# A four-layer graph network: VectorE's order in the last layers, the bias adds, and the exps of the last group of a chunk

## The chip, the core and the metric

The kernel runs on one core of one Trainium2 chip. The metric is the device time of one execution in microseconds (us); the profile is of one execution, taken by the hardware profiler. The engines are called PE (TensorE's matmuls) and PEld (its weight loads), DVE (VectorE), ACT (ScalarE), POOL (GpSimd) and SP (SyncE, which here only issues DMAs).

## The reference

A graph of 3327 nodes with 128 features, and a dense adjacency matrix `adj` (3327 x 3327). Four layers, each with a residual and a layer norm:

```python
# layer 0: attention, d = 128 features act as the batch, 8 heads inside, adj added to the scores twice
q = (x @ Wq.T).reshape(d, n, h); k = (x @ Wk.T).reshape(d, n, h); v = (x @ Wv.T).reshape(d, n, h)
a = softmax(einsum('dnh,dmh->dnm', q, k) * d ** -0.5 + adj + adj, axis=2)
x = layernorm(x + einsum('dnm,dmh->dnh', a, v).reshape(n, h * d) @ Wo.T)
# layer 1
dinv = sum(adj + I, axis=1) ** -0.5
x = layernorm(x + (dinv[:, None] * (adj + I) * dinv[None, :]) @ (x @ W1.T + b1))
# layer 2: rows of adj and of adj.T, each divided by its sum where that is positive
x = layernorm(x + norm(adj) @ x @ W_in + norm(adj.T) @ x @ W_out)
# layer 3
x = layernorm(x + x @ W_self.T + (adj @ x) @ W_neigh.T + b3)
```

## The kernel before, in words

**Attention** (0 to 9798 us of the profiled execution, after a set-up of some 320 us). The queries are cut into 7 chunks of 476 columns (`CW`), the keys into 4 key blocks of 7, 7, 6 and 6 tiles of 128 (`KBS`); one block of the program is one chunk with one key block, 28 in all. In each block a loop runs over the 128 features `d`, in groups of four (`GROUP`). A step of it makes the scores of one `d` in three sets of two or three key tiles: PE writes them to PSUM (`sc`, line 740), and `exponents` takes exp of them. ACT does most of it (line 745). Where `on_vector(b, d, si)` says so, the last tile of the set is left to DVE, which has no exp and does a chain of seven instructions instead (`vector_exp`, lines 630 to 647; the first, line 634, reads the scores from PSUM into `ey`). The table `SHARE` names the sets, by (3d + si) mod 36; 2072 of the 10752 sets have such a chain. `weigh` (line 780) multiplies the exps by the values; `flush` (line 794) adds the sums to `acc`. The orders of PE, ACT, POOL and DVE are written out in the source here (`tc.manual_schedule`): `take` decides, with costs and due times, which of DVE's pieces (first step of a chain, next step, flush, copy of queries) is traced next. In a chunk's first block DVE copies the queries of each group one group ahead (`copy_queries`, lines 538 to 540); for the first group this falls in the last group of the chunk before.

**The last layers** (9804 us to the end) work on 26 tiles `t` of 128 nodes.

- A first loop divides the attention's sums and projects them. `divide(t)` loads the tile `o` (SP), takes the reciprocal `rec` (DVE, line 1263) and multiplies it in (`on`, line 1265: POOL, DVE for t = 0). `stage0(t)` then has `heads_turned(t)` (8 transposes on PE, line 1273, copied by ACT), `outputs(t - 1)` (16 matmuls, line 1282; `h` on DVE, line 1285; the layer norm, with its last step on ACT), `turn(t - 3)` (a transpose, line 1214, copied by ACT) and `support(t - 4)` (the projection with `w1T`, line 1222, scaled by ACT into `y1`).
- Layer 1 gathers: for each `t` a tile `eT` of the transposed adjacency is loaded (1664 KB, five buffers) and 26 tokens' worth of matmuls, two each, accumulate in PSUM (line 1247). Between them, at fixed places, stand `turn(t - 1)` and `messages(t - 1)`, which need the norm of the tile before. Behind a gather come `z`, `h` and `norm` on DVE, then `add_columns(t)`: DVE sums the tile's columns (`part`, line 1229), from which layer 2's divisors are made.
- Layer 2 first multiplies by the adjacency itself (line 1353), then gathers again (10295 to 10478 us), with `back` and `last_inputs(t - 1)` between the matmuls; layer 3 gathers a third time and stores.

`project` adds the bias of layers 1 and 3 as a second matmul into the same PSUM bank: a row of ones against the bias row (line 1224; fp32 matmuls of this kind are issued as two instructions).

In the last layers `manual_schedule` names PE and SP: these two follow the source. The order of DVE, ACT and POOL is left to the framework's scheduler, so it can differ from the source's.

Of the kernel before, what the change touches and what calls it, by code (L numbers as in the profile page):

```python
# [10 lines left out]
F32 = mybir.dt.float32  # L11
# [3 lines left out]
ALU = mybir.AluOpType  # L15
# [4 lines left out]
P = 128  # L20
GROUP = 4
# [30 lines left out]
def kernel(ctx: ExitStack, tc: tile.TileContext, x, adj, wq, wk, wv, wo,  # L52
# [14 lines left out]
    nc = tc.nc  # L67
    N, D = x.shape
# [12 lines left out]
    KBS = [(0, 7), (7, 7), (14, 6), (20, 6)]  # L81
    assert KBS[-1][0] + KBS[-1][1] == T

    def tokens(t):
        return P - 1 if t == T - 1 else P

    def load_rows(eng, sb, dram, t):
        for a, n in spans(tokens(t)):
            eng.dma_start(out=sb[a:a + n, :], in_=dram[t * P + a:t * P + a + n, :])
# [5 lines left out]
    def flat_ap(dram, at, pattern):  # L95

        f = dram.rearrange("r c -> (r c)")
        if isinstance(at, int):
            base = f[at:at + 1]
        else:  # L100
            base = f[ds(at, 1)]
        return bass.AP(base.tensor, base.offset, pattern)

    const = ctx.enter_context(tc.tile_pool(name="const", bufs=1))
# [1 line left out]

    ident = const.tile([P, P], F32, name="ident")
    make_identity(nc, ident)
    ones_row = const.tile([1, P], F32, name="ones_row")
    nc.gpsimd.memset(ones_row, 1.0)  # L110
    eps = const.tile([P, 1], F32, name="eps")
    nc.gpsimd.memset(eps, EPS)

# [144 lines left out]
    with tc.tile_pool(name="pw", bufs=1) as pw, tc.tile_pool(name="pa", bufs=2) as pa, \  # L258
# [12 lines left out]
        for u in range(NU):  # L271
# [4 lines left out]
            for a, n in ([(0, P)] if full == P else [(0, 112), (112, full - 112)]):  # L276
                nc.sync.dma_start(out=xr[a:a + n, 0:R, :],
                                  in_=flat_ap(x, (base + R * a) * D, [[R * D, n], [1, R * D]]))
            if rest:
                nc.sync.dma_start(out=xr[full:full + 1, 0:rest, :],  # L280
                                  in_=flat_ap(x, (base + R * full) * D, [[D, 1], [1, rest * D]]))
            ps = pps.tile([P, 4, P], F32, tag="ps", bufs=3, name="xtr")
# [108 lines left out]
        d = 0  # L391
# [20 lines left out]
    def attention():  # L412
        with tc.tile_pool(name="ed", bufs=1) as ed, tc.tile_pool(name="kq", bufs=3) as kq, \
# [14 lines left out]
            blocks = [(min(c, N - CW), kb) for c in range(0, N, CW) for kb in range(len(KBS))]  # L428
# [3 lines left out]
            def load_edges(b, j):  # L432
# [15 lines left out]
            SHARE = {  # L448
                0: (8, 13, 20, 27, 32, 35),
                7: (5, 8, 12, 20, 23, 29, 32, 35),  # L450
                6: (4, 8, 13, 19, 25, 31, 35),
            }
# [25 lines left out]
            def kind(b):  # L478
                kb = blocks[b][1]
                return KBS[kb][1] if kb else 0  # L480

            def on_vector(b, d, si):
                return (3 * d + si) % 36 in SHARE[kind(b)]

            FIRST = {7: (4, 4, 5, 7, 7, 10, 10), 6: (4, 4, 7, 7, 10, 10)}

# [659 lines left out]
    act = ctx.enter_context(tc.tile_pool(name="act", bufs=1))  # L1146
    small = ctx.enter_context(tc.tile_pool(name="small", bufs=4))
    big = ctx.enter_context(tc.tile_pool(name="big", bufs=5))
    work = ctx.enter_context(tc.tile_pool(name="work", bufs=3))
    banks = ctx.enter_context(tc.tile_pool(name="banks", bufs=1, space=PSUM))  # L1150
    xs = [act.tile([P, T, D], F32, name=f"x{i}") for i in range(2)]
    y1 = act.tile([P, T, D], F32, name="y1")
# [3 lines left out]
    def bank(i):  # L1156
        return banks.tile([P, 512], F32, tag=f"bank{i}", name=f"bank{i}")

    w1T, w2, w3T, woT = (act.tile([P, w], F32, name=f"tw{i}") for i, w in enumerate((D, 2 * D, 2 * D, HD)))
# [1 line left out]
        nc.scalar.dma_start(out=sb, in_=dram)  # L1161
    nc.scalar.dma_start(out=w2[:, 0:D], in_=w2_in)
    nc.scalar.dma_start(out=w2[:, D:2 * D], in_=w2_out)
    b1_sb = act.tile([1, D], F32, name="b1_sb")
    nc.scalar.dma_start(out=b1_sb, in_=b1.unsqueeze(0))
    b3_sb = act.tile([1, D], F32, name="b3_sb")
    nc.scalar.dma_start(out=b3_sb, in_=b3.unsqueeze(0))


    for i in range(4):  # L1170
# [3 lines left out]
    dinv = act.tile([P, T], F32, name="dinv")  # L1174
# [33 lines left out]
    xTs = {}  # L1208
# [6 lines left out]
        xTs[t] = work.tile([P, P], F32, name="xT")  # L1215
        nc.scalar.copy(xTs[t][:, :n], ps[:, :n])

    def project(t, w, bias, b):

        n = tokens(t)  # L1220
        ps = bank(b)
        nc.tensor.matmul(ps[:n, 0:w.shape[-1]], lhsT=xTs[t][:, :n], rhs=w, start=True, stop=bias is None)  # L1222
        if bias is not None:
            nc.tensor.matmul(ps[:n, 0:D], lhsT=ones_row[:, :n], rhs=bias, start=False, stop=True)  # L1224
        return ps

    def add_columns(t):
# [39 lines left out]
    def heads_turned(t):  # L1267
        n = tokens(t)
        oTs[t] = work.tile([P, H, P], F32, name="oT")
        for c in range(0, H, 4):  # L1270
            ps = bank(c // 4).rearrange("p (c n) -> p c n", n=P)
            for i in range(4):
                nc.tensor.transpose(ps[:, i, :n], ons[t][:n, c + i, :], ident[:n, :n])  # L1273
            nc.scalar.copy(oTs[t][:, c:c + 4, :n], ps[:, :, :n])
# [12 lines left out]

    def support(t):
        n = tokens(t)
        ps = project(t, w1T, b1_sb, 5)  # L1290
        nc.scalar.mul(y1[:n, t, :], ps[:n, 0:D], dinv[:n, t:t + 1])

    def messages(t):
        n = tokens(t)
        ps = project(t, w2, None, 5)
        nc.scalar.copy(y2[:n, t, :], ps[:n, 0:2 * D])

    def last_inputs(t):
        n = tokens(t)
        ps = project(t, w3T, b3_sb, 5)  # L1300
        nc.vector.tensor_tensor(xs[1][:n, t, :], ps[:n, 0:D], xs[0][:n, t, :], ALU.add)
        nc.scalar.copy(y3[:n, t, :], ps[:n, D:2 * D])

    with tc.manual_schedule(engines={mybir.EngineType.PE, mybir.EngineType.SP}):
        def stage0(t):
            if t < T:
                heads_turned(t)
            if 1 <= t <= T:
                outputs(t - 1)
            if 3 <= t <= T + 2:  # L1310
                turn(xs[0], t - 3, 4)
            if 4 <= t <= T + 3:
                support(t - 4)

        for t in range(T):
            divide(t)
            stage0(t)


        def after(src, t, finish):  # L1320
            return [(12, lambda: turn(src, t, 4)), (19, lambda: finish(t))] if t >= 0 else []

        for t in range(T):
            n = tokens(t)
            ps = gather(t, y1, 0, 6 + t % 2,
                        after(xs[1], t - 1, messages) if t else
                        [(2 + 5 * k, lambda k=k: stage0(T + k)) for k in range(4)])
            z = work.tile([P, D], F32, name="z")
            nc.vector.tensor_tensor(z[:n, :], ps[:n, 0:D], y1[:n, t, :], ALU.add)
            h = work.tile([P, D], F32, name="h")  # L1330
            nc.vector.scalar_tensor_tensor(h[:n, :], z[:n, :], dinv[:n, t:t + 1], xs[0][:n, t, :],  # L1331
                                           ALU.mult, ALU.add)
            norm(n, h[:n, :], xs[1][:n, t, :])
            add_columns(t)
        inv_col = inverse_degree(colsum, "inv_col")


        backT = act.tile([P, NP], F32, name="backT")
        cols = [(c, min(512, N - c)) for c in range(0, N, 512)]
        order = [6, 0, 1, 2, 3, 4, 5]  # L1340
        acc = {}
        for t in range(T):
            n = tokens(t)
            a = big.tile([P, T * P], F32, tag="big", name="a2")
            load_rows(nc.sync, a[:, 0:N], adj, t)
            for i, (c, w) in enumerate(cols):
                if t == 0 and i == 3:
                    turn(xs[1], T - 1, 4)
                if t == 0 and i == 5:
                    messages(T - 1)  # L1350
                if t == 0:
                    acc[i] = bank(order[i])
                nc.tensor.matmul(acc[i][:, 0:w], lhsT=y2[:n, t, D:2 * D], rhs=a[:n, c:c + w],  # L1353
                                 start=(t == 0), stop=(t == T - 1))
        for i, (c, w) in enumerate(cols):
            copy(i, backT[:, c:c + w], acc[i][:, 0:w])


        for t in range(T):
            n = tokens(t)  # L1360
            zs = {}

            def back(t=t, n=n):
                pb = bank(t % 2)
                nc.tensor.transpose(pb[:n, 0:P], backT[:, t * P:t * P + n], ident)
                zs[t] = work.tile([P, D], F32, name="z")
                nc.vector.scalar_tensor_tensor(zs[t][:n, :], pb[:n, 0:D], inv_col[:n, t:t + 1], xs[1][:n, t, :],
                                               ALU.mult, ALU.add)

            ps = gather(t, y2, 0, 7 - t % 2, [(6, back)] + after(xs[0], t - 1, last_inputs))  # L1370
            h = work.tile([P, D], F32, name="h")
            nc.vector.scalar_tensor_tensor(h[:n, :], ps[:n, 0:D], inv_row[:n, t:t + 1], zs[t][:n, :],  # L1372
                                           ALU.mult, ALU.add)
            norm(n, h[:n, :], xs[0][:n, t, :])


        for t in range(T):
            n = tokens(t)
            ps = gather(t, y3, 0, 6 + t % 2, after(xs[0], T - 1, last_inputs) if t == 0 else ())
            h = work.tile([P, D], F32, name="h")  # L1380
            nc.vector.tensor_tensor(h[:n, :], ps[:n, 0:D], xs[1][:n, t, :], ALU.add)
            res = work.tile([P, D], F32, name="res")
            norm(n, h[:n, :], res[:n, :])
            store_rows(nc.gpsimd, out, res, t)
# [29 lines left out]
```

## Time and profile before

| | us |
|---|---|
| three timed runs | 10636.44, 10639.43, 10634.66; median 10636.44 |
| profiled execution | 10646.07 |
| its span, first to last instruction | 10644.3 |
| attention ends (last flush) | 9797.95 |
| first `heads_turned` of the last layers | 9811.28 |
| last `heads_turned` | 9902.21 |
| layer 1's gathers end | 10149.31 |
| layer 2's gathers, from and to | 10295 to 10478 |
| last gather ends | 10630.5 |

The stretches add up along the span, so what a stage gains or loses is read as the move of the next stage's start. Over the span PE is busy 98%, ACT 89%, DVE 86% and POOL 15%; a busy PE is not one at its peak, since matmuls are pipelined and their ends are modelled. The line PEclk, and the clock in a table of stretches, is the share of TensorE's full clock that was granted; over the span it is 0.991. In a timeline, a bracket behind an instruction gives the idle time of its engine before it and what ended it. The chain of work that ended last runs through PE for most of its length in the last layers; in layer 1 it goes from `eT` loads to column sums (`part`) to PE, turn by turn.

The forms that the change touches: the first instruction of a DVE chain (line 634) takes 651 ns; ACT's exp takes 613 ns for one tile, 999 for two and 1397 for three; the one-row matmul instructions (line 1224) are 104, mean 321 ns; `rec` takes 951 ns, POOL's `on` 2357, a column sum 3616.

### The profile page before, as it was taken

The page shows a single profiled execution, that of the slowest core. Times are in us where ns is not written, and L with a number is a line of the kernel's source. Part 1 is how long each engine was busy: PE and PEld are TensorE (multiplying, and loading weights), DVE is VectorE, ACT ScalarE, POOL GpSimd, SP SyncE. Part 2 cuts the span into 40 slices and gives each one's busy share as a digit, 9 for nine tenths or more (in the row PEclk, how much of TensorE's full clock was granted, in tenths as well). Part 3 has the DMA queues.
Part 4 walks back from the last instruction along what each step waited for, and adds up shares of the span by engine and source line. Part 5 has one row for each costly group of instructions (what it writes and reads, how often), then busy time and mean ns, then how long its engine had stood idle before and what let it go on. Part 6 is the DMA issues. An engine that isn't in the chain of part 4 may idle for free. (4 is left out here: it accounts for less than half of the span.)

```text
span 10644.3 us, 209858 instructions
## 1 busy us (share of the span) xinstructions
PE 10442.3 (98%) x76939; PEld 4077.7 (38%) x76939; DVE 9138.5 (86%) x16662; ACT 9447.3 (89%) x11231; POOL 1615.6 (15%) x2734
## 2 busy tenths in 40 slices
PE   8899999999999999999999999999999999999899
PEld 5333333333333333333333333333333333333869
DVE  6789999899998999989999999999899998998512
ACT  3899999999999999999999999999999999998200
POOL 0111222111121111111111111111111110001100
PEclk9999999999999999999999999999999999999899
DMA  7678996789976899769997688886889868887576
GB/s 269 189 185 195 214 218 180 181 196 207 214 185 175 199 206 213 187 172 202 207 213 189 168 196 198 201 194 162 198 204 212 195 165 189 191 194 181 196 276 238
DMA packets 1013655, 2117.00 MB, mean 199 GB/s; under 512 B 206535, under 2 KB 730833, under 8 KB 998803
## 3 DMA queue, kind: packets, MB, share of 16 engines
q1 hardware_dynamic: 932054, 1985.62, 76.7%
q0 software_dynamic: 79136, 116.02, 3.6%
q8 instruction: 622, 10.19, 0.4%
q14 instruction: 407, 3.33, 0.1%
q10 hardware_dynamic: 1436, 1.84, 0.1%
HBM read 1863.03 MB, written 239.54 MB: 198 GB/s over the span
## 5 line engine op out<-in xcount | busy, mean ns | idle before, releaser
L745 ACT ACTIVATE e<-sc 128x952 f32<-128x952 f32 (+2 forms) x10752 | 9223.9, 991 | 274.5 <-PE sc L740 202.3
L780 PE MATMUL o<-e,v_pad 128*32 128x476 f32 (+1 forms) x46592 | 5671.5, 574 | 9.2 <-POOL v_pad L554 7.1
L740 PE MATMUL sc<-qt,kt 64*128 64x476 f32 x23296 | 4312.0, 436 | 61.9 <-DVE ey L634 40.1
L740 PEld LDWEIGHTS sc<-qt,kt 64*128 64x128 f32 x23296 | 2131.7, 184 | 4286.9 <-ACT e L745 2583.3
L644 DVE SCALAR_TENSOR_TENSOR e<-e,ey 128x476 f32<-128x476 f32 x4144 | 2669.2, 651 | 36.4
L634 DVE TENSOR_SCALAR ey<-sc 128x476 int32<-128x476 f32 x2072 | 1348.1, 651 | 574.5 <-ACT e L745 541.6
L780 PEld LDWEIGHTS o<-e,v_pad 128*32 128x32 f32 (+1 forms) x46592 | 1032.9, 108 | 1928.3 <-issue 1900.5
L554 POOL COPY v_pad<-vs 128x192 f32<-128x192 f32 (+1 forms) x896 | 536.9, 621 | 7770.5 <-DMA vs<-v_img 6360.7
L644 DVE SCALAR_TENSOR_TENSOR e<-ey 128x476 f32<-128x476 f32 x2072 | 1344.5, 652 | 28.5
L644 DVE SCALAR_TENSOR_TENSOR e<-e,et 128x476 f32<-128x476 f32 x2072 | 1346.2, 652 | 7.7
L638 DVE TENSOR_SCALAR et<-ey 128x476 int32<-128x476 int32 x2072 | 847.9, 412 | 11.0
L641 DVE TENSOR_SCALAR ey<-ey 128x476 int32<-128x476 int32 x2072 | 841.3, 409 | 13.9
L244 POOL DMA_DIRECT2D adjT_s<-at x1352 | 747.3, 561 | 166.2 <-DMA adjT_s<-at 128.3
L1247 PE MATMUL bank<-y,eT 128*128 128x128 f32 (+1 forms) x4056 | 496.6, 283 | 0.4 <-DVE h L1372 0.4
L1247 PEld LDWEIGHTS bank<-y,eT 128*128 128x128 f32 (+1 forms) x4056 | 488.9, 199 | 6.6 <-DVE h L1372 0.6
L1199 ACT ACTIVATE rstd<-mv,eps 128x1 f32<-128x1 f32 x104 | 30.5, 293 | 315.5 <-DVE mv L1197 315.5
L540 DVE CAST qt<-qt 64x1904 fp32r<-64x1904 f32 x224 | 258.9, 1156 | 7.4
L794 DVE TENSOR_TENSOR acc<-o,acc 128x476 f32<-128x476 f32 x231 | 150.9, 653 | 97.8 <-PE o L780 96.2
L538 DVE TENSOR_SCALAR qt<-qt 32x1428 fp32r<-32x1428 f32 x224 | 202.2, 903 | 24.8 <-DMA qt<-q_s 18.5
L802 POOL DMA_DIRECT2D o_s<-acc x304 | 186.1, 616 | 17.5 <-issue 8.8
L1353 PE MATMUL bank<-a,y 128*128 128x512 f32 (+2 forms) x364 | 145.5, 561 | 0.0
L1229 DVE TENSOR_REDUCE part<-eT 128x26 f32<-128x3328 f32 x25 | 90.4, 3616 | 54.7 <-DMA eT<-adjT_s 54.6
(143 smaller groups left out, 2220.0 us busy)
## 6 DMA issues: line engine op xcount, KB each, us to landing
qt<-qimg SPq DMA_DIRECT2D x1344, 476.0 KB
kt<-k_s SPq DMA_DIRECT2D x5316, 96.0 KB
kt<-k_s SPq DMA_DIRECT2D x1762, 128.0 KB
eT<-adjT_s SPq DMA_DIRECT2D x78, 1664.0 KB
qimg<-qt SPq DMA_DIRECT2D x224, 476.0 KB
vs<-v_img SPq DMA_DIRECT2D x224, 224.0 KB
adjT_s<-at POOLq DMA_DIRECT2D x1352, 32.0 KB
vs<-v_img SPq DMA_DIRECT2D x224, 192.0 KB
```

The costliest lines, as they stand in the source:

```text
L244: nc.gpsimd.dma_start(out=flat_ap(adjT_s, (t * P + 32 * q) * NP + c * PIECE, [[NP, 32], [P, ns], [1, P]]), in_=at[32 * i:32 * i + 32].rear ...
L538: return [(0.9, lambda: nc.vector.tensor_scalar(qt[32:64, 1:], qf[0:32, 0:GROUP - 1], -1.0, None, ALU.mult)), (0.42, lambda: nc.vector.ten ...
L540: (1.17, lambda: nc.vector.tensor_copy(qt[64:128], qf[0:64]))]
L554: nc.gpsimd.tensor_copy(vp[:, 32:32 + nt * GROUP * 32].rearrange("p (x c) -> p x c", c=32)[:, :, 0:H], vs.rearrange("p (x c) -> p x c", c=H))
L634: nc.vector.tensor_scalar(yi, x, -58 * math.log(2.0), 2 ** 24 / math.log(2.0), ALU.max, ALU.mult)
L638: nc.vector.tensor_scalar(parts["t"].bitcast(I32), yi, UPPER, EXPONENT, ALU.bitwise_and, ALU.bitwise_xor)
L641: nc.vector.tensor_scalar(yi, yi, LOWER, QUARTER, ALU.bitwise_and, ALU.bitwise_or)
L644: nc.vector.scalar_tensor_tensor(e, e if i else y, POLY[i], parts["t"] if i == len(POLY) - 1 else y, ALU.add, ALU.mult)
L740: nc.tensor.matmul(s[:, i, 0:CW], lhsT=kt[64 * rg:64 * rg + 64, k, pos * P:(pos + 1) * P], rhs=qt[64 * rg:64 * rg + 64, k, :], start=False ...
L745: nc.scalar.activation(e[:, 0:own, :], s[:, 0:own, 0:CW], AF.Exp, bias=-2 * PHASE, scale=2.0)
L780: nc.tensor.matmul(o[32 * j:32 * j + 32, 0:CW], lhsT=values[b, g][:m, c:c + 32], rhs=es[b, g * GROUP + j, r][:m, :], start=first and u == ...
L1247: nc.tensor.matmul(ps[:n, 0:D], lhsT=e[:m, s, :n], rhs=y[:m, s, col:col + D], start=(s == 0), stop=(s == T - 1))
```

## The change

Three parts.

1. In the last layers DVE joins the engines whose instructions follow the source. No line is moved, and the loops stay as they are.
2. `project` has no bias any more. `support` and `last_inputs` add it with a DVE instruction of its own, from the projection's PSUM bank into a new tile `lin`, and go on from `lin`; the biases are loaded into all 128 partitions. The row of ones is gone.
3. `on_vector` is false in the last group (d = 124 to 127) of each chunk's last key block: ACT does these exps.

```diff
-                return (3 * d + si) % 36 in SHARE[kind(b)]
+                return (3 * d + si) % 36 in SHARE[kind(b)] and (blocks[b][1] != len(KBS) - 1 or d < D - GROUP)
...
-    b1_sb = act.tile([1, D], F32, name="b1_sb")
-    nc.scalar.dma_start(out=b1_sb, in_=b1.unsqueeze(0))
-    b3_sb = act.tile([1, D], F32, name="b3_sb")
-    nc.scalar.dma_start(out=b3_sb, in_=b3.unsqueeze(0))
+    b1_sb, b3_sb = (act.tile([P, D], F32, name=f"b{i}_sb") for i in (1, 3))
+    for sb, dram in ((b1_sb, b1), (b3_sb, b3)):
+        nc.scalar.dma_start(out=sb, in_=bass.AP(dram.tensor, dram.offset, [[0, P], [1, D]]))
...
-    def project(t, w, bias, b):
+    def project(t, w, b):
...
-        nc.tensor.matmul(ps[:n, 0:w.shape[-1]], lhsT=xTs[t][:, :n], rhs=w, start=True, stop=bias is None)
-        if bias is not None:
-            nc.tensor.matmul(ps[:n, 0:D], lhsT=ones_row[:, :n], rhs=bias, start=False, stop=True)
+        nc.tensor.matmul(ps[:n, 0:w.shape[-1]], lhsT=xTs[t][:, :n], rhs=w, start=True, stop=True)
...
     def support(t):
         n = tokens(t)
-        ps = project(t, w1T, b1_sb, 5)
-        nc.scalar.mul(y1[:n, t, :], ps[:n, 0:D], dinv[:n, t:t + 1])
+        ps = project(t, w1T, 5)
+        lin = work.tile([P, D], F32, name="lin")
+        nc.vector.tensor_tensor(lin[:n, :], ps[:n, 0:D], b1_sb[:n, :], ALU.add)
+        nc.scalar.mul(y1[:n, t, :], lin[:n, :], dinv[:n, t:t + 1])
...
     def last_inputs(t):
         n = tokens(t)
-        ps = project(t, w3T, b3_sb, 5)
-        nc.vector.tensor_tensor(xs[1][:n, t, :], ps[:n, 0:D], xs[0][:n, t, :], ALU.add)
+        ps = project(t, w3T, 5)
+        lin = work.tile([P, D], F32, name="lin")
+        nc.vector.tensor_tensor(lin[:n, :], ps[:n, 0:D], b3_sb[:n, :], ALU.add)
+        nc.vector.tensor_tensor(xs[1][:n, t, :], lin[:n, :], xs[0][:n, t, :], ALU.add)
         nc.scalar.copy(y3[:n, t, :], ps[:n, D:2 * D])
 
-    with tc.manual_schedule(engines={mybir.EngineType.PE, mybir.EngineType.SP}):
+    with tc.manual_schedule(engines={mybir.EngineType.PE, mybir.EngineType.SP, mybir.EngineType.DVE}):
```

## The prediction

> **What bounds the kernel now.** I read the page's first part, then the busy time by stage, then the timeline on each side of every place that the change touches. Columns of the second fence: stretch and its length, busy us (and instructions) of PE, PEld, DVE, ACT and POOL, granted clock, DMA share, GB/s.
>
> ```profile
> PE 10442.3 (98%) x76939; PEld 4077.7 (38%) x76939; DVE 9138.5 (86%) x16662; ACT 9447.3 (89%) x11231; POOL 1615.6 (15%) x2734
> ```
>
> ```profile
> 9831.00:9902.00 71.00, 70.92 (x579) 66.21 (x580) 38.35 (x121) 46.32 (x119) 47.18 (x21) 1.00 0.72 204
> ...
> 9917.00:10149.50 232.50, 187.45 (x1379) 182.99 (x1378) 124.73 (x203) 23.34 (x75) 0.00 (x0) 0.87 0.51 185
> ...
> 10295.00:10478.00 183.00, 182.67 (x1504) 171.16 (x1502) 48.26 (x178) 20.96 (x76) 0.00 (x0) 1.00 0.67 244
> ```
>
> TensorE (PE) is busy nearly everywhere, so what counts is where it waits. The first last-layer stage (9831 to 9902) and the layer-2 gathers (10295 to 10478) have no idle PE; there only PE work shortens the time. The layer-1 gathers (9917 to 10149.5) leave PE idle 45 of 232.5 us, and the clock falls to 0.87.
>
> **Part A, VectorE in source order, first stage.** One step of the loop today (timeline, all engines):
>
> ```profile
> 9863.09 1.09 PE L1273 MATMUL bank<-ident,on 128*128 128x128 f32 x8
> ...
> 9864.02 1.95 PE L1282 MATMUL bank<-tw,oT 128*128 128x128 f32 x16
> 9864.07 0.95 DVE L1263 RECIPROCAL rec<-o 128x128 f32<-128x128 f32 x1 [0.78 <-DMA o<-o_s]
> ...
> 9865.16 2.36 POOL L1265 TENSOR_TENSOR on<-o,rec 128x1024 f32<-128x1024 f32 x1 [1.39 <-DVE rstd L1200]
> ...
> 9866.01 0.29 DVE L1285 TENSOR_TENSOR h<-bank,xt 128x128 f32<-128x128 f32 x1 [0.71 <-PE bank L1282]
> ```
>
> VectorE (DVE) now takes `rec` of a later tile as soon as its load lands, before the `h` of this step. In source order `rec(t+1)` stands behind `h(t-1)`, its norm and the new add of `support(t-4)`. But `h(t-1)` waits for PE's `outputs(t-1)`, which PE does after `heads_turned(t)`; and `heads_turned(t+1)` waits for `on(t+1)` on POOL, which waits for `rec(t+1)`. What overlapped becomes one ring. Queued behind the waiting `h` on DVE are the norm, the add and `rec`; POOL, then PE, wait for them.
>
> Its length: heads turned to outputs 0.93, outputs to `h` 1.99 (9863.09, 9864.02, 9866.01). `h` to `off`: 1.40, as the same five instructions take in the last stage (`h` 10491.18, fifth instruction 10492.58). `off` 0.24 to its successor (9837.32 to 9837.56), the new add 0.33 (a 128x128 add from PSUM starts its successor that much later, 10491.18 to 10491.50). `rec` 0.95, 0.09 to POOL, 2.36, 0.04 to PE. Sum 8.33 us, against 3.56 now (9863.09 to 9866.65).
>
> Then the clock. PE works 3.2 us of the ring and idles 5.1. The stage of today's gaps shows what idling does (same columns as above, stretches of 3.41 us):
>
> ```profile
> 9930.37:9933.79 3.42, 1.18 (x11) 0.99 (x9) 3.42 (x4) 0.09 (x1) 0.00 (x0) 1.00 0.89 366
> 9933.79:9937.20 3.41, 3.03 (x14) 3.04 (x15) 2.01 (x3) 0.27 (x1) 0.00 (x0) 0.50 0.19 78
> ```
>
> The clock changes on a grid of 3.41 us. A window with PE busy for 0.34 is followed by half clock, and it stays until a window is nearly full (the second line's 0.89 was enough, 0.86 at a chunk end was not). A gap of 5.1 us leaves, wherever the grid falls, a window idle for at least 2.55 us, busy 0.25 at most. So PE resumes at half clock in each step and keeps it for 3.41 to 6.83 us: the 2.72 us of heads turned and outputs grow by 1.7 to 2.7. Following the grid by these rules through 23 steps I get 10.3 us a step.
>
> The third `heads_turned` comes at 9825.9: `h(0)` at 9820.78 as now, then 1.40 + 0.24 + 0.95 + 0.09 + 2.36 + 0.04. The last, 23 steps later, comes at 10063 instead of 9902.21: **+160 us** (+115 without half clock, +178 with all PE work of a step at half clock). Removing the one-row matmuls gives nothing here: PE waits for the ring.
>
> [...] The rows above show half clock after a window that was a third busy, and the sum goes by the rows.
>
> **Part B, source order in the layer-1 gathers.** Today DVE and PE do this (two timelines):
>
> ```profile
> 9946.62 3.62 DVE L1229 TENSOR_REDUCE part<-eT 128x26 f32<-128x3328 f32 x1 [4.97 <-DMA eT<-adjT_s]
> 9950.16 0.28 DVE L1329 TENSOR_TENSOR z<-bank,y 128x128 f32<-128x128 f32 x1
> ```
>
> ```profile
> 9952.34 0.48 PE L1214 MATMUL bank<-ident,x 128*128 128x128 f32 x1 [3.82 <-DVE x L1206]
> ...
> 10141.01 0.60 PE L1222 MATMUL bank<-tw,xT 128*128 128x256 f32 x2
> ...
> 10147.33 0.60 PE L1222 MATMUL bank<-tw,xT 128*128 128x256 f32 x2
> ```
>
> The column sum of a tile that has not landed stands ahead of the norm of a gather that is done; PE waits for the norm. In source order the sum follows the norm, of a tile that landed long ago. The step is then PE's own: 6.32 us, as between the last two lines, where nothing waits. DVE needs about 5.7 of it (`z` to `x` 2.0, sum 3.62). `x` is ready 2.0 us after a gather, PE asks for it after 24 matmuls of 0.112, 2.7. The buffer is free 5.5 us later than PE's last read, but five buffers are four steps ahead. From the last `heads_turned` to the end of the gathers: 4.5 for the stage's rest (3.55 now, part at half clock) + 9.6 for the first gather (11.25 now, less four one-row pairs at 0.41) + 25 x 6.32 = 172. Now it is 9902.21 to 10149.31, 247. **-75 us**; if loads or DVE held it at layer 2's present step of 7.07, -56.
>
> **Part C, biases.** A one-row pair costs PE what follows (timeline of PE in layer 2):
>
> ```profile
> 10305.32 0.60 PE L1222 MATMUL bank<-tw,xT 128*128 128x256 f32 x2
> 10305.85 0.48 PE L1224 MATMUL bank<-b_sb,ones_row 1*128 1x128 f32 x2
> 10306.26 3.17 PE L1247 MATMUL bank<-y,eT 128*128 128x128 f32 x26
> ```
>
> Projection to next matmul is 0.94 with the pair and 0.43 without (10147.33 to 10147.76): 26 x 0.51 = **-13 us** (-11 at 0.41). The 26 added DVE adds of 0.29 in layer 2 hide in a DVE that is idle 135 of 183 us; without that cover they would cost 7.5. The two bias loads grow from one row to 128 rows; issue times of the 128-row weight loads beside them are 0.35 to 0.47 us, so ScalarE's queue moves by -0.3 to +0.3 us. They are wanted four tiles later: 0. The dropped memset of 0.19 us lies in the set-up: 0.
>
> **Part D, no exps on DVE in the last four steps of a chunk.** Fourteen chains go (2 x 7). Those of d = 124 and 126 (rows 13 and 19 of the share) read their scores late, since DVE is busy with the next chunk's query copies (DVE, then PE):
>
> ```profile
> 3031.82 0.64 DVE L634 TENSOR_SCALAR ey<-sc 128x476 int32<-128x476 f32 x1
> ```
>
> ```profile
> 3032.52 1.16 PE L740 MATMUL sc<-qt,kt 64*128 64x476 f32 x4 [2.63 <-DVE ey L634]
> ```
>
> At the six inner chunk ends this wait is 3.78, 2.63, 2.38, 2.42, 2.76 and 2.68: 16.7 us. Eight windows at half clock follow, in which PE makes 1.57 us of progress in 2.83: 8 x 3.41 x 0.45 = 12. ScalarE takes over 14 single exps; two exps in one instruction take 0.999 against 0.613, so 0.39 each, 5.4 in all, mostly in time in which it now waits for PE. **-24 us**; from +5 (the wait moves to the copies, ScalarE pays) to -29.
>
> **Sum.** +160 - 75 - 13 - 24 = +48. It is made against the profiled execution, 10646.07 us with a span of 10644.3, 10 above the runs' median of 10636.44. Carried to the median: **10685 us**.
>
> **Rivals.**
> 1. *The ring runs at full clock*: +115 - 112 = +3, 10640. This is the other side, and the place is the ring alone: the third `heads_turned` is 5.4 us later (9825.9 against 9820.5), and 23 steps of ring less 3.56 make up the rest, so that the 112 us of parts B to D pay for it at a ring of 3.56 + (112 - 5.4) / 23 = 8.2 us; from there down the kernel is not slower. Against it: every PE gap over 2.5 us in the stretches that I read is followed by half clock. Chance 0.08.
> 2. *`rec` still runs ahead*, because the order does not bind it: no ring, 22 x -0.41 in its place, 10636 - 9 - 112 = 10515. Against it: PE and SP, which are under source order now, keep it exactly (heads turned, outputs, turn, projection; `o`, then `xt`). Chance 0.07.
> 3. *Layer 1 gets a new bound*: DVE has 0.6 us to spare in a step, and a late tile now delays norms too. At 7.07 a step 10704, at today's 9.3 10760. For it: in the chain of waits today's loads take 6.8 to 7.9 us from release to landing. Against it: the last stage loads a tile each 5.81 us. Chance 0.13.
> 4. *The chunk-end wait moves* to the copies or to ScalarE: part D from 0 to +5, 10709 to 10714. Chance 0.12.
>
> The main case keeps 0.60, its own range 10665 to 10710 (half clock +150 to +175, part D -15 to -29). The range for 8 in 10 takes in rivals 3 and 4 and the edge of 1: 10640 to 10740. A difference of 0.2%, 21 us, is about what can be told from none. Faster 0.08 (rival 2 and a hundredth), same 0.08 (rival 1 and the low tail), slower 0.84.
>
> **What would show it.** In the first stage: `rec` directly behind the new add, PE idle about 5 us a step on POOL's `on`, a clock near 0.6, steps of 10 us. In layer 1: column sums behind the norm, no PE wait, clock 1.00, steps of 6.3. In layer 2: steps of 6.56 instead of 7.07. At chunk ends: no PE wait on `ey` above 1 us. The prediction is wrong if `rec` is seen ahead of `h`, if the ring's clock is 1.00, or if layer 1 waits for loads.

## The result and the profile after

The changed kernel takes 10685.52 us (median of 5 runs, 10683.66 to 10692.01), the kernel before 10634.66 (5 runs, 10623.96 to 10639.43). The ratio, estimated from all of these runs, is 1.0051, with a 95% interval of 1.0036 to 1.0065: slower by half a per cent. One run of the kernel before among those of the experiments, 13416.89 us at a granted clock of 0.653, is in no comparison. The profiled execution spans 10689.9 us, 45.6 more than before. Stage by stage, in the two profiled executions (first PE instruction of a stage to that of the next, unless said otherwise):

| stage | before, us | after, us | change | forecast |
|---|---|---|---|---|
| start to the last `weigh` of the attention | 9797.25 | 9772.45 | -24.8 | -24 (D) |
| to the first `heads_turned` | 14.03 | 14.22 | +0.2 | 0 |
| to the last `heads_turned` | 90.93 | 250.86 | +159.9 | +160 (A, with the line above) |
| to the end of layer 1's gathers | 247.10 | 173.23 | -73.9 | -75 (B) |
| layer 2's product with `adj`, layers 2 and 3, to the last gather's end | 481.14 | 465.26 | -15.9 | -13 (C) |
| tail | 13.8 | 13.8 | 0 | 0 |

From the page's first part, after:

```profile
PE 10435.8 (98%) x76835; PEld 4092.9 (38%) x76835; DVE 9107.7 (85%) x16616; ACT 9455.6 (88%) x11231; POOL 1626.1 (15%) x2733
```

Over the whole span the shares are what they were, so the page's first lines would not have told one kernel from the other. The busy time by stage of the changed kernel, with the columns of before (busy us and instructions of PE, PEld, DVE, ACT, POOL; clock; DMA share; GB/s): the first last-layer stage, layer 1's gathers, layer 2's.

```profile
9801.00:10037.00 236.00, 123.84 (x616) 119.16 (x615) 50.27 (x159) 57.04 (x135) 53.34 (x23) 0.67 0.29 88
10037.00:10211.00 174.00, 173.12 (x1482) 171.56 (x1483) 137.04 (x215) 28.80 (x90) 0.48 (x1) 0.99 0.67 245
10358.00:10519.00 161.00, 161.00 (x1400) 159.77 (x1400) 53.77 (x198) 20.15 (x73) 0.00 (x0) 1.00 0.73 266
```

The first stage was 71 us of unbroken PE at full clock; now PE is busy for half of 236 us, at a clock of 0.67. The 45 us of idle PE in layer 1 are gone. One step of the first stage (timeline, weight loads, DMA issues and some of ACT and DVE left out):

```profile
9930.59 0.18 DVE L1194 BATCH_NORM_AGGREGATE mv<-st 128x2 f32<-128x6 f32 x1
...
9931.34 0.21 DVE L1200 TENSOR_SCALAR off<-mv,rstd 128x1 f32<-128x1 f32 x1
9931.47 0.28 DVE L1287 TENSOR_TENSOR lin<-bank,b_sb 128x128 f32<-128x128 f32 x1
...
9931.67 0.94 DVE L1258 RECIPROCAL rec<-o 128x128 f32<-128x128 f32 x1
...
9932.74 2.34 POOL L1260 TENSOR_TENSOR on<-o,rec 128x1024 f32<-128x1024 f32 x1 [7.90 <-DVE rec L1258]
9935.13 1.97 PE L1268 MATMUL bank<-ident,on 128*128 128x128 f32 x8 [4.90 <-POOL on L1260]
...
9936.89 3.25 PE L1277 MATMUL bank<-tw,oT 128*128 128x128 f32 x16
...
9940.18 0.29 DVE L1280 TENSOR_TENSOR h<-bank,xt 128x128 f32<-128x128 f32 x1 [7.57 <-PE bank L1277]
```

This is the ring, link by link: norm, add, `rec`, POOL's `on`, heads turned, outputs, `h`, and round again. The brackets tell who waits for whom: POOL for `rec` 7.9 us, PE for `on` 4.9, DVE for the outputs 7.6. The eight transposes take 1.97 us against 1.09 before, the sixteen matmuls 3.25 against 1.95: half clock (the granted clock was 0.50 from 9932.79 to 9939.61 us). From the ninth step on the steps are 10.24 to 10.28 us, nearly all of them 10.24.

In layer 1 the column sum now stands behind the norm (timeline of DVE, after):

```profile
10103.09 0.29 DVE L1328 TENSOR_TENSOR z<-bank,y 128x128 f32<-128x128 f32 x1 [0.47 <-PE bank L1242]
...
10104.88 0.35 DVE L1203 TENSOR_SCALAR x<-h,mv,rstd 128x128 f32<-128x128 f32 x1
10105.14 3.61 DVE L1224 TENSOR_REDUCE part<-eT 128x26 f32<-128x3328 f32 x1
```

`x` is there 2.1 us after `z` starts. PE asks for it 0.34 us later and does not wait; its line has no bracket (timeline of PE, after):

```profile
10105.57 0.27 PE L1211 MATMUL bank<-ident,x 128*128 128x128 f32 x1
```

In layer 2 the matmuls follow the projection directly (timeline of PE, after):

```profile
10405.50 0.60 PE L1219 MATMUL bank<-tw,xT 128*128 128x256 f32 x2
10405.94 2.28 PE L1242 MATMUL bank<-y,eT 128*128 128x128 f32 x19
```

That is 0.44 us from one to the other, where it was 0.94. From one projection to the next it is now 6.46 us, where it was 7.07. At the chunk end shown before (2980 to 3050 us), PE's waits on the scores add up to this (waiter, releaser, us in total, times, the longest):

```profile
PE sc L738 <- DVE ey L632: 0.5, 2, 0.3
```

### The profile page after: what moved, and what is told of

Same layout as the page of the kernel before. It is cut to its first block, busy times and chain, and to the rows that moved or that the text cites. A ratio compares the mean times of both kernels' runs of the same rounds, so it can differ in the third digit from the quotient of the medians.

```text
span 10689.9 us, 209547 instructions
## 1 busy us (share of the span) xinstructions
PE 10435.8 (98%) x76835; PEld 4092.9 (38%) x76835; DVE 9107.7 (85%) x16616; ACT 9455.6 (88%) x11231; POOL 1626.1 (15%) x2733
## 3 DMA queue, kind: packets, MB, share of 16 engines
q10 hardware_dynamic: 1720, 1.97, 0.1%
## 5 line engine op out<-in xcount | busy, mean ns | idle before, releaser
L1242 PE MATMUL bank<-y,eT 128*128 128x128 f32 (+1 forms) x4056 | 470.6, 275 | 0.4 <-DVE h L1371 0.4
L1242 PEld LDWEIGHTS bank<-y,eT 128*128 128x128 f32 (+1 forms) x4056 | 467.5, 192 | 3.3 <-DVE h L1371 0.6
L792 DVE TENSOR_TENSOR acc<-o,acc 128x476 f32<-128x476 f32 x231 | 151.0, 654 | 105.0 <-PE o L778 103.2
L1268 PE MATMUL bank<-ident,on 128*128 128x128 f32 (+1 forms) x208 | 51.1, 427 | 133.7 <-POOL on L1260 119.5
```

What stands on the lines that cost most here:

```text
L1242: nc.tensor.matmul(ps[:n, 0:D], lhsT=e[:m, s, :n], rhs=y[:m, s, col:col + D], start=(s == 0), stop=(s == T - 1))
```

## The experiments

All times of the stages below are from the profiled executions, measured as in the table. "Two ahead" is e4.

**e1: the order alone.** The kernel before, with one edit:

```diff
-    with tc.manual_schedule(engines={mybir.EngineType.PE, mybir.EngineType.SP}):
+    with tc.manual_schedule(engines={mybir.EngineType.PE, mybir.EngineType.SP, mybir.EngineType.DVE}):
```

> Only VectorE's source order in the last layers; biases stay one-row matmuls, exps as before. Ring theory: attention ends as before (near 9797 us); the first stage's step is the ring without the new add, 8.0 us at full clock, 10.0 to 10.4 with half clock, so the last heads_turned comes 155 to 160 us later than before; layer 1's gathers take 175 us from there instead of 247; layer 2's step stays 7.07. Total about +85, 10720 us. Rival (the new adds, not the order, lengthen the stage): the step stays at 3.55 us and the order alone gives -74, 10560 us.

Measured: 10731.27 us (one run; before 10635.13 on the same chip), 11 more than expected; between the profiled executions the difference is 85.2 us, as forecast. From the attention's end to the last `heads_turned` 263.8 us against 105.0 before (+158.8), from there through layer 1 175.7. The step settles at 10.24 us. So the order alone makes parts A and B; the adds don't make the ring. It is told below why a ring without the add is no shorter.

**e2: the exps alone.** The kernel before with the new `on_vector`.

> Only the exps of the last group of a chunk go to ScalarE. My theory: no wait of TensorE on ey above 1 us at the six inner chunk ends, no half-clock windows behind them, attention ends 25 us earlier (9772 us), and all of it reaches the end: 10610 us. Rival (the wait moves to the query copies or to ScalarE, which pays 14 x 0.39 us): attention ends between 9797 and 9803, 10635 to 10640 us.

Measured: 10620.25 us (one run; before 10635.13 on the same chip), 10 more than expected; span 10618.2, the attention's end at 9774.4. The longest wait of PE on `ey` at the second to sixth chunk ends is 0.4 us. Both profiles have one longer than that at the first end, 0.7 here and 1.1 in the changed kernel, where it was 3.8. The attention's end moves by some us from run to run whatever is changed (9791.2 in e3, 9795.0 in e1, 9797.3 before, which share that code), so I measured the six inner chunk ends by themselves: from the 60th score matmul ahead of the border to the 27th behind it. Their sum is 255.7, 254.1, 253.0 and 248.8 us in the four profiles with the old exps (before, e1, e3, e10), and 229.9 to 232.7 in the eight with the new. The mean difference is 22 us, against 24 forecast. The end of the attention itself, in the same profiles, moves by less: 9791.2 to 9797.3 with the old exps and 9772.5 to 9784.4 with the new, 17 us between the means, so the eight take some 5 us more elsewhere in the attention. The rival, that the whole wait moves to the copies or to ScalarE, falls; that some 5 us of it do is not excluded.

**e3: the biases alone.** The changed kernel's `project`, `support` and `last_inputs`, with DVE's order left to the scheduler and the old exps.

> Only the biases move to VectorE; its order stays the scheduler's. My theory: the first stage is bound by TensorE, so its step falls from 3.55 to 3.14 us (-10 in all), layer 2's step from 7.07 to 6.46 (-16), layer 1 stays near 247 less 2: 10608 us. Rival (the adds cost VectorE time on the path): the first stage's step stays 3.55 or grows and only layer 2 gains, 10620 us or more.

Measured: 10622.22 us (one run), 14 more than I expected. Layers 2 and 3 gain 15.9 us, as forecast. The first stage gains 3 and not 10: its steps are uneven, 3.05 us and 3.3 to 5.0 in turn, mean 3.44. In the last 15 steps PE waits for `on` in every other one, 0.15 to 1.45 us; there `rec` had started late, in all but one after 1.8 to 3.1 us in which DVE stood idle and which the landing of `o` ended. In this timeline of e3 the first `rec` (tile 14) starts early, PE waits for the `on` of tile 13, and the second `rec` (tile 15) starts late:

```profile
9850.69 0.95 DVE L1258 RECIPROCAL rec<-o 128x128 f32<-128x128 f32 x1 [0.65 <-DMA o<-o_s]
...
9851.51 1.09 PE L1268 MATMUL bank<-ident,on 128*128 128x128 f32 x8 [0.23 <-POOL on L1260]
...
9854.95 0.95 DVE L1258 RECIPROCAL rec<-o 128x128 f32<-128x128 f32 x1 [1.90 <-DMA o<-o_s]
```

Layer 1 stays at 248.0. The time is the rival's (10620 us or more), but its reason, adds on the path, is not shown: what comes late is the load of `o`. Why it lands late in every other step stays open.

**e4: two tiles ahead.** The changed kernel, with `divide` traced earlier:

```diff
         for t in range(T):
-            divide(t)
+            if t + 2 < T:
+                divide(t + 2)
             stage0(t)
```

(`divide(0)` and `divide(1)` stand ahead of the loop.)

> The changed kernel with one edit: divide(t + 2) is traced ahead of stage0(t), so that rec stands two tiles ahead in VectorE's order. Ring theory: the ring of 8.3 us is spread over three steps (2.8 each), TensorE's own 3.14 us decides, clock 1.00; the last heads_turned comes 165 to 170 us earlier than in the changed kernel and the rest stays: 10517 us. Rival (the stage is slow through VectorE's or GpSimd's own time, or through the adds, whatever the place of rec): the step stays above 8 us and the time near 10685.

Measured: 10517.07 us (4 runs, 10509.02 to 10520.17), ratio to the kernel before 0.9888 (0.9871 to 0.9904). The stage's step is 2.99 us and every later one is the same. The timeline of e4 (other lines left out):

```profile
9830.40 1.04 PE L1268 MATMUL bank<-ident,on 128*128 128x128 f32 x8
...
9831.99 0.94 DVE L1258 RECIPROCAL rec<-o 128x128 f32<-128x128 f32 x1
...
9833.07 2.37 POOL L1260 TENSOR_TENSOR on<-o,rec 128x1024 f32<-128x1024 f32 x1 [0.63 <-DVE rec L1258]
...
9833.39 1.04 PE L1268 MATMUL bank<-ident,on 128*128 128x128 f32 x8
```

The same `rec` behind the same add, and the same `on`, but PE turns heads without a wait: this `on` is for the tile two steps after the first line's. The edit moves one call and no arithmetic, and by the medians 168 us are back. The ring theory stands; its rival, that the engines' own time makes the stage, falls. This version beats both kernels.

**e5: one tile ahead.**

> As two tiles ahead, but divide(t + 1) ahead of stage0(t), one tile. Ring theory: 8.3 us are now spread over two steps, 4.2 us a step; TensorE idles 1.2 of them, too little for half clock, so the clock stays 1.00 and the last heads_turned comes 25 to 28 us later than with two tiles ahead, 10544 us. Rival (any rec ahead of h is enough, TensorE then decides): 2.99 us a step and 10517.

Measured: 10558.88 us (one run), 15 more than expected. The stage takes 128.3 us from the attention's end, 37.5 more than two ahead; 27 were expected. Two steps together take 8.12 us where the clock is full (5.07 and 3.05), as the ring shared by two would have it, but 9.75 (5.07 and 4.68) elsewhere: the clock of the stage is 0.90, with windows at half clock that I had excluded. The order of the three versions (10.29, 4.54 and 2.97 us a step on average) is what the ring asks for; that the clock stays full at one ahead was wrong: that 1.2 us of idle PE a step are too little for half clock was my estimate, and this run does not bear it out.

**e6 and e9: PE kept busy.** In the changed kernel PE gets 18 more matmuls behind each `support`, in e6 each on its own, in e9 as one accumulation group:

```diff
             stage0(t)
+            fill = bank(7)
+            for i in range(18 if 1 <= t < T - 1 else 0):
+                nc.tensor.matmul(fill[:, 0:P], lhsT=ident, rhs=woT[:, 0:P], start=(i == 0), stop=(i == 17))
```

> The changed kernel, in whose first stage TensorE does 18 more fp32 128x128 matmuls (36 instructions, 4.0 us at full clock) into an unused bank behind each support, from t = 1 to 24; nobody reads them. Clock theory: they fill most of the 5 us gap, the clock stays 1.00, heads turned and outputs take 2.72 us instead of 5.4, and the step is the ring at full clock, 8.3 to 8.5 us: 45 us less than the changed kernel, 10640. Rival (the 10.3 us are latencies, the clock adds nothing): the step stays at 10.3; second rival (the filler gets in the way of heads_turned): more than 10.3.

Measured: 10752.39 us (one run), 12.5 us a step. The second rival: each pair, a group of its own, waits for the pair before it in the bank, so the filler takes 9.68 us and not 4, and PE comes late to `heads_turned`. The timeline of e6:

```profile
9840.37 9.68 PE L1318 MATMUL bank<-tw,ident 128*128 128x128 f32 x36
9840.81 0.30 PEld L1318 LDWEIGHTS bank<-tw,ident 128*128 128x128 f32 x2 [0.25 <-PE bank L1318]
9841.36 0.30 PEld L1318 LDWEIGHTS bank<-tw,ident 128*128 128x128 f32 x2 [0.25 <-PE bank L1318]
```

The weight loads, two at a time, start 0.55 us apart, each behind a wait for the matmul before. This says nothing of the clock, so e9 does it in one group.

> e6 again with the 18 matmuls as one accumulation group, so that none waits for the one before it: 36 instructions in a row, 4.0 us at full clock, from t = 1 to 24; nobody reads them. Clock theory: TensorE is busy 7.2 of the ring's 8.3 us, the clock stays 1.00, the step is 8.3 to 8.5 us and the last heads_turned comes 42 to 45 us earlier than in the changed kernel, 10641 us. Rival (10.24 us, three of the clock's windows, is set by latencies and not by the clock): the step stays at 10.2 and the time at 10685.

Measured: 10643.73 us (one run), 8.12 us a step. The stretch of e9 with the same columns as above, and a step of it:

```profile
9810.00:9990.00 180.00, 160.33 (x1399) 156.16 (x1398) 48.64 (x154) 53.00 (x132) 52.66 (x23) 1.00 0.35 106
```

```profile
9902.01 1.09 PE L1268 MATMUL bank<-ident,on 128*128 128x128 f32 x8 [0.89 <-POOL on L1260]
...
9902.95 1.95 PE L1277 MATMUL bank<-tw,oT 128*128 128x128 f32 x16
...
9904.93 0.29 DVE L1280 TENSOR_TENSOR h<-bank,xt 128x128 f32<-128x128 f32 x1 [5.45 <-PE bank L1277]
...
9905.07 4.18 PE L1319 MATMUL bank<-tw,ident 128*128 128x128 f32 x36
...
9906.46 0.28 DVE L1287 TENSOR_TENSOR lin<-bank,b_sb 128x128 f32<-128x128 f32 x1
...
9906.66 0.94 DVE L1258 RECIPROCAL rec<-o 128x128 f32<-128x128 f32 x1
```

More work on PE makes the kernel 42 us faster: the ring is the same, but the clock is 1.00 and the PE part of it takes its 2.9 us. It also measures the prediction's first rival, the ring at full clock: 10643.73, beside 10633.85 to 10647.64 for six runs of the kernel before on that chip. At full clock the change would have come out level; half clock makes it slower.

**e7: the column sum first.** Two ahead, with `add_columns(t)` traced ahead of `norm` in layer 1:

```diff
-            norm(n, h[:n, :], xs[1][:n, t, :])
             add_columns(t)
+            norm(n, h[:n, :], xs[1][:n, t, :])
```

> Two tiles ahead, and in layer 1 the column sum of a tile is traced ahead of that tile's norm instead of behind it. My theory of layer 1 (the sum's place ahead of the norm holds TensorE up): x is ready 5.9 us after a gather where TensorE asks after 2.7, so each step waits 3.2 us: 9.5 us a step, up to 11 with half clock, 80 to 120 us more than two tiles ahead, 10597 to 10640. Rival (only the sums of tiles that had not landed cost, by VectorE's wait for the load): no load is waited for here, so the step stays 6.3 to 7 and the time 10517 to 10535.

Measured: 10663.61 us (one run). From the last `heads_turned` through layer 1 305.7 us against 171.0 two ahead, +135, somewhat more than my upper end. PE's timeline in e7:

```profile
9931.64 0.33 PE L1211 MATMUL bank<-ident,x 128*128 128x128 f32 x1 [3.17 <-DVE x L1203]
9931.81 3.15 PE L1242 MATMUL bank<-y,eT 128*128 128x128 f32 x14
...
9943.02 0.48 PE L1211 MATMUL bank<-ident,x 128*128 128x128 f32 x1 [3.17 <-DVE x L1203]
```

The wait is 3.17 us a step, as worked out; the fourteen matmuls behind it take 3.15 us where they took 1.73 at full clock (layer 2 of the kernel before), and the stage's clock is 0.81. No load is waited for. So the sum's place ahead of the norm is by itself enough to hold PE up, and moving it behind the norm is what part B does. In the kernel before, DVE also waited for tiles that had not landed, 54.6 us in layer 1; how much of the 74 us is that wait and how much the sum's own time, the runs do not split.

**e8: source order from layer 1 on only.** The changed kernel, with DVE's order the scheduler's in the first stage and the source's from there on (a second `manual_schedule` block).

> The changed kernel with VectorE in source order from layer 1 on only; the first stage's VectorE order is the scheduler's, biases added by VectorE. If the two stages are independent: the first stage as with the biases alone (3.44 us a step, uneven, 88 us from first to last heads_turned), layer 1 as in the changed kernel (173 us): 10528 us. Rival (source order in layer 1 needs it in the stage before, through the buffers or the loads): layer 1 above 185 us, 10540 or more.

Measured: 10529.88 us (4 runs, 10518.55 to 10536.7; 10528 expected), ratio to the kernel before 0.9893 (0.9876 to 0.9909). The first stage's steps are 3.39 us on average. With two blocks PE's order is no longer one either: the first matmuls of layer 1 start within the first stage, at 9817.0. So the split between the two stages can't be read as in the other runs. From the attention's end to the end of layer 1 it takes 271.1 us, against 261.8 two ahead and 438.3 in the changed kernel. So A can be left out and B kept: layer 1 steps at 6.35 us here too, without a wait.

**e10: two ahead, old exps.**

> Two tiles ahead, with the exps of the last group back on VectorE: part D alone is undone. My theory: the six waits of 2.4 to 3.8 us at the chunk ends and the half clock behind them come back, 17 to 25 us: 10534 to 10542. Rival (the attention absorbs them elsewhere in a chunk): within 5 us of 10517.

Measured: 10553.65 us (4 runs, 10539.39 to 10554.59), 12 above the expected range; ratio to the kernel before 0.9918 (0.9900 to 0.9936). The profiled executions differ by 21.2 us, the six chunk ends by 18.4. By the ratios it is 0.3% (some 32 us) behind two ahead, measured on another occasion and with intervals that touch. Part D's gain reaches the end; its size lies between 15 us (e2 against the kernel before on its chip) and these 32.

## Why the prediction was right, point by point

- **Part A** was right in mechanism and size: 10.3 us a step forecast, 10.29 measured, +160 in both. The size came out of two parts. The ring at full clock was put at 8.33 us; e9 has 8.12, since `off` starts its successor 0.13 us later, not 0.24, and the add 0.20, not 0.33. Half clock was put at 2.0 us a step; 10.24 less 8.12 is 2.1. The two misses cancel. That the steps would lock to exactly three windows was not foreseen, and the prediction's reading of the windows does not settle every case: in the kernel before, half clock stayed behind a window in which PE was busy for 0.96 (8834.72 to 8838.13 us), in the changed one it ended behind one at 0.83 (9792.85 to 9796.27), and one tile ahead (e5) a full clock was expected, and half clock came in part of the steps. That the step was hit so closely has some luck in it; that half clock comes in every step has not.
- **Part B** was right: -75 forecast, -73.9 measured, step 6.35 us against 6.32. e7 shows that the sum's place alone can hold PE up, e8 that part B needs nothing of part A.
- **Part C** was 3 us short: the step of layer 2 fell from 7.07 to 6.46 us, 0.61 a pair and not 0.51; 26 times that is the 15.9 measured. I took the pair from the stretch between two starts and stopped at the first matmul behind it, but with the pair that matmul, too, holds its successor up: 0.21 us from start to start against 0.11 without. The 26 adds did hide, as the unbroken PE of that stage shows.
- **Part D** was right: -24 forecast, -24.8 in the pair of the table; over all profiles -22 at the six chunk ends and -17 at the attention's end, within the stated -15 to -29.
- **The rivals.** The first, a ring at full clock, is what e9 builds, and its 10640 lies 4 us from what e9 measures. The second, `rec` staying ahead, did not come. The third did not either: the gathers of layer 1 run without a PE wait and at 0.99. The fourth fell in e2, but for the 5 us told there.
- **The carry to the median**: the profiled execution before lay 10 us above its median; the changed one, 10692.01, lies 6.5 above. This and the small misses cancel to within a microsecond of 10685.52, which is luck: the attention's end alone moves by 6 to 12 us between profiles that share its code.

Put together: the change held three gains worth 115 us by the table and one loss of 160, and the loss is the trace order of one line. The change asked for source order where the source had never been written as an order.

## What to carry to other kernels

When an engine goes from a scheduler's order to the source's, go through each loop and ask which instruction starts the next step's chain, and whether it stands behind one that waits for the end of this step: a producer that feeds the step through other engines must be traced so far ahead that the ring, spread over one step more than it is ahead, is shorter than the bounding engine's step (here 8.1 us over three steps against 3.0). Source order pays where long, patient work, such as these column sums, would otherwise get ahead of a short chain that the bounding engine waits for. And look at the granted clock where a ring leaves TensorE idle; here half clock made a fifth of the step (2.1 of 10.24 us, the changed kernel beside e9).

## What the runs showed of the hardware

The stage's steps locked to the windows of the granted clock. In the changed kernel's trace that clock was half for 6.83 us and full for 3.41, in turn, from 9799.7 to 10042.0 us. Four windows of 3.41 us along these borders (columns as above; the clock is the third from the end):

```profile
9932.79:9936.20 3.41, 1.07 (x5) 1.07 (x6) 0.00 (x0) 0.00 (x0) 2.29 (x1) 0.50 0.00 2
9936.20:9939.61 3.41, 3.41 (x18) 3.41 (x17) 0.00 (x0) 1.17 (x2) 0.00 (x0) 0.50 0.62 171
9939.61:9943.03 3.42, 0.86 (x8) 0.67 (x6) 2.20 (x7) 1.34 (x4) 0.05 (x1) 1.00 0.07 22
9943.03:9946.44 3.41, 1.06 (x5) 1.07 (x6) 0.00 (x0) 0.00 (x0) 2.29 (x1) 0.50 0.00 1
```

Two windows at half clock, one at full, and so on to the stage's end: three windows are 10.24 us, and that is the step. In the window at full clock PE ends its step within the first 0.9 us and idles for the rest, so that it is a quarter busy, and half clock follows. Heads are turned late in the first window at half clock (PE busy 1.07 of 3.41 us); the second is full of work (3.41 us), and full clock comes behind it, when the work is nearly over. So the 10.24 us are no sum of latencies. e1, whose ring is shorter by the add (0.20 us in e9), settles at the same 10.24. A fifth of a microsecond more or less in the ring changed nothing; 4 us of matmuls that nobody reads took 2.1 us off it (8.12 in e9). In each step a window at full clock in which PE was busy for a quarter or less was followed by half clock.

No one busy share of PE divides the windows that full clock followed from those that half clock followed. Four windows of e5, along its grid:

```profile
9843.15:9846.57 3.42, 1.51 (x14) 1.47 (x14) 1.96 (x7) 1.14 (x4) 2.77 (x2) 1.00 0.05 6
9846.57:9849.98 3.41, 3.41 (x33) 3.41 (x32) 1.49 (x7) 2.38 (x7) 1.50 (x1) 1.00 0.73 201
9849.98:9853.39 3.41, 1.53 (x14) 1.34 (x13) 2.59 (x8) 1.41 (x5) 2.35 (x1) 1.00 0.64 182
9853.39:9856.81 3.42, 3.42 (x18) 3.42 (x18) 0.32 (x1) 1.74 (x4) 2.35 (x1) 0.50 0.63 176
```

PE is busy 1.51 us in the first and 1.53 in the third; full clock follows the one and half clock the other, the busier of the two.
